# Where a graph layer's logarithms are taken: one activation over four tiles, or two inside an earlier stage

## The chip, the cores and the metric

The kernel runs on one core of a Trainium2 chip, in float32 for all large products. The metric is the device time of one execution in microseconds. A core has TensorE (PE, matmuls; its weight loads are listed apart as PEld), VectorE (DVE), ScalarE (ACT), GpSimd (POOL, which here mostly issues accumulating transfers), and SyncE (SP), which issues most of the transfers. Each engine works through its own instructions in the order in which they were written; engines wait for each other through semaphores.

## The reference

Two graph attention layers over 512 nodes, 768 features and 16,896 edges, the first with eight heads whose outputs are concatenated, then a residual sum and a layer norm. Cut to what matters:

```python
def gat_layer(x, W, a_s, a_d, b, edge_index, concat):
    h = (x @ W).reshape(n, H, C)
    src, dst = (edge_index[0], edge_index[1])
    alpha_s = jnp.einsum('nhc,hc->nh', h, a_s)
    alpha_d = jnp.einsum('nhc,hc->nh', h, a_d)
    e = jax.nn.leaky_relu(alpha_s[src] + alpha_d[dst], 0.2)
    m = jax.ops.segment_max(e, dst, num_segments=n)
    e = jnp.exp(e - m[dst])
    denom = jax.ops.segment_sum(e, dst, num_segments=n)
    alpha = e / (denom[dst] + 1e-16)
    out = jax.ops.segment_sum(h[src] * alpha[:, :, None], dst, num_segments=n)
    return out.reshape(n, H * C) + b
h = jax.nn.elu(gat_layer(x, W1, a_src1, a_dst1, b1, ...))   # 8 heads of 768
y = gat_layer(h, W2, a_src2, a_dst2, b2, ...)               # 1 head
return layernorm(x + y)
```

## The kernel before, in words

The graph becomes a dense 512 x 512 matrix of edge counts, built once with one-hot matmuls (L681) while head 0's projection runs. `cnt` holds it in four tiles of 128 destinations x 512 sources, `absent` a large number wherever a pair has no edge. Attention is then dense: for each tile, a row of logits (`lift`, L575, on ScalarE), the leaky ReLU (`leak`, L579, VectorE), the row minimum with the mask (`rank`, L584, VectorE) and the exponential (L588 or L590, ScalarE).

Head 0 multiplies the exponentials by the counts (`weigh`, L811). All later heads have the counts inside the exponent: `logarithms` (L596) replaces all of `cnt` by the logarithm of itself plus a tiny number, and `fold_count` (L601, VectorE) turns a tile into `absent` minus the logarithm. From then on `folded` is not empty, and `rank` adds `cnt` instead of `absent` and lets the exponential sum up the denominator as well.

The first layer runs head by head. Each head has three stages: `projection` (x times the head's W1; `by_thirds` in later heads), `mixed` (the aggregation, attention times projected features), and `second` (ELU of the aggregate times the head's rows of W2, summed up in `h2`). The products use Strassen-like schemes of seven parts, P1 to P7. In `second` each part has two halves of 128 rows, and each half takes six matmul records (L367), so a part takes twelve. P2 accumulates onto the PSUM banks of P1, P4 onto those of P7 and P3 onto those of P5, after `empty` has taken the first part out: for head 0 with copies on ScalarE (L458) for P1 and P2, on VectorE for P6 (L462), P7 and P4 (L460).

In the loop over `n` from 2 to 6 inside a head (P6, P7, P4, P5, P3), the matmuls m0 and m1 of part n are written first, then `leak` and `rank` of the next head's attention tile n - 2, the next tile's `lift`, then e0 and e1, which empty the banks, with `weigh` and `turn_out` of finished attention tiles between. `turn_out` (L831 and L834, ScalarE, and a transposing transfer at L836 on SP) and `turn_in` (L839, ScalarE) transpose the attention into `PT`.

Head 0's stages around the change: projection 1 ends (`beside`, n = 13) with `turn_in(3)` and the sums over `PT` that the aggregation needs (L883 to L886, VectorE). `mixed` then runs three rounds c = 0, 1, 2; each copies P1 out into u (L915, ScalarE), adds P6 and P7 (L919, L920), passes P2 to `elu` (two Relus, L848 and L849, and an Exp, L850, on ScalarE, then L851 on VectorE), subtracts w from P5 (L925), adds P4 (L928) and P3 (L930), with logits of the next head (L376) in between. P3's matmuls accumulate onto P5's bank and so wait for L925. L360 is the last of the sums that P4's weights need in `second`.

ScalarE evaluates functions from a table set. A load of another set (`ACT_TABLE_LOAD` in the profile) stands ahead of the first activation that needs it: ahead of L596 for the logarithm, ahead of the first L588 after it for the exponential, and ahead of L1279 for the square root.

Of the kernel before, what the change touches and what calls it, by code (L numbers as in the profile page):

```python
# [13 lines left out]
AF = mybir.ActivationFunctionType  # L14
# [23 lines left out]
def gat_pass(  # L38
# [16 lines left out]
    nc = tc.nc  # L55
# [4 lines left out]
    NT = N // P  # L60
# [192 lines left out]
    tiny = const.tile([P, 1], F32, name="tiny")  # L253
# [73 lines left out]
    cnt = keep.tile([P, NT, N], F32, name="cnt")  # L327
# [244 lines left out]
    def lift(h, t):  # L572

        q = BC[h] if 0 < h < H and t + 1 == NT else qpool.tile([P, N], F32, name="q")
        nc.scalar.activation(q, BC[h][:, :N], AF.Identity, bias=AL[h][1][:, t:t + 1], scale=-1.0)  # L575
        return q

    def leak(q):
        nc.vector.scalar_tensor_tensor(q, q, NEG_SLOPE, q, op0=ALU.mult, op1=ALU.min)  # L579

    def rank(q, t):

        nmax = small.tile([P, 1], F32, name="nmax")
        nc.vector.tensor_tensor_reduce(out=q, in0=q, in1=(cnt if folded else absent)[:, t, :], scale=1.0,  # L584
                                       scalar=-NO_EDGE / 2 if folded else -NO_EDGE, op0=ALU.add, op1=ALU.min, accum_out=nmax)
        if folded:
            dens[t] = small.tile([P, 1], F32, name="den")
            nc.scalar.activation(q, q, AF.Exp, bias=nmax, scale=-1.0, accum_out=dens[t])  # L588
        else:
            nc.scalar.activation(q, q, AF.Exp, bias=nmax, scale=-1.0)  # L590
        return q

    folded, dens = [], {}

    def logarithms():
        nc.scalar.activation(cnt, cnt, AF.Ln, bias=tiny)  # L596
        folded.append(True)

    def fold_count(t):

        nc.vector.tensor_tensor(cnt[:, t, :], absent[:, t, :], cnt[:, t, :], op=ALU.subtract)  # L601
# [15 lines left out]
    if not general:  # L617
# [12 lines left out]
        cps, done = {}, set()  # L630
# [207 lines left out]
    def turn_in(t):  # L838
        nc.scalar.copy(PT.rearrange("p s n -> p (s n)").bitcast(U16).rearrange("p (s n h) -> p s n h", s=NT, h=2)[  # L839
            :, :, t * P:(t + 1) * P, :], parted.pop(t).rearrange("p (h s d) -> p s d h", h=2, s=NT))  # L840

    def elu(h, c, z, cols, name, spare=None):

        j = h * DC + c
        n = z.shape[-1]
        neg = work.tile([P, n], F32, name=f"n{name}")
        pos = work.tile([P, n], F32, name=f"z{name}", bufs=3 if name == "r" else 2) if spare is None else spare
        nc.scalar.activation(neg, z, AF.Relu, bias=nb1T[:, j:j + 1], scale=-1.0)  # L848
        nc.scalar.activation(pos, z, AF.Relu, bias=b1T[:, j:j + 1])  # L849
        nc.scalar.activation(neg, neg, AF.Exp, scale=-1.0)  # L850
        return lambda: nc.vector.scalar_tensor_tensor(gT[:, c, cols], neg, -1.0, pos, op0=ALU.add, op1=ALU.add)  # L851
# [13 lines left out]
    def left_sums(h):  # L865
        hs = HS[h]
        a11, a12, a21, a22 = hs[:, :2, L], hs[:, 2:, L], hs[:, :2, R], hs[:, 2:, R]
        s1, s2, s4 = (gS.rearrange("p a k n -> p a (k n)")[:, j, :].rearrange("p (k n) -> p k n", k=2)
                      for j in range(3))
        tt = nc.vector.tensor_tensor  # L870
        return dict(P1=a11, P2=a12, P3=s4, P4=a22, P5=s1, P6=s2, P7=a21), [
            lambda: tt(s1, a21, a22, op=ALU.subtract),
            lambda: tt(s2, s1, a11, op=ALU.subtract),
            lambda: tt(a21, a11, a21, op=ALU.subtract),
            lambda: tt(s4, a12, s2, op=ALU.add),
        ]

    def right_sums():
        b11, b12, b21, b22 = PT[:, :2, near], PT[:, :2, far_], PT[:, 2:, near], PT[:, 2:, far_]
        t1, t2, t4 = pS[:, 0], pS[:, 1], pS[:, 2]  # L880
        tt = nc.vector.tensor_tensor
        return dict(P1=b11, P2=b21, P3=b22, P4=t4, P5=t1, P6=t2, P7=b12), [
            lambda: tt(t1, b11, b12, op=ALU.add),  # L883
            lambda: tt(t2, t1, b22, op=ALU.add),
            lambda: tt(b12, b12, b22, op=ALU.add),
            lambda: tt(t4, t2, b21, op=ALU.add),  # L886
        ]

    def mixed(h, A_, B_, fill):

        tt = nc.vector.tensor_tensor
        behind = []

        def some(n):
            for f in fill[:n]:
                f()
            del fill[:n]

        for c in range(HK):
            u = work.tile([P, HN], F32, name="u")  # L900
            w = work.tile([P, HN], F32, name="w")
            zr = work.tile([P, N], F32, name="zr", bufs=3)
            bank = {}

            def part(p, over=None):
                if over is None:
                    bank[p] = mm.tile([P, 512], F32, name="mm")
                else:
                    bank[p] = bank[over]
                for k in range(2):  # L910
                    nc.tensor.matmul(bank[p][:, :HN], A_[p][:, k, c * P:(c + 1) * P], B_[p][:, k, :],  # L911
                                     start=over is None and k == 0, stop=k == 1, skip_group_check=True)
                return bank[p][:, :HN]

            nc.scalar.copy(u, part("P1"))  # L915
            if behind:

                behind = behind[0]()
            tt(u, u, part("P6"), op=ALU.add)  # L919
            tt(w, u, part("P7"), op=ALU.add)  # L920
            for f in behind[:1]:
                f()
            near_l = elu(h, c, part("P2", over="P1"), near, "l")
            some(1)
            tt(zr[:, far_], part("P5"), w, op=ALU.subtract)  # L925
            for f in behind[1:]:
                f()
            tt(zr[:, near], u, part("P4", over="P7"), op=ALU.add)  # L928
            near_l()
            tt(u, part("P3", over="P5"), u, op=ALU.subtract)  # L930
            some(-(-len(fill) // (2 * (HK - c) - 1)))

            def others(c=c, u=u, zr=zr):
                return [elu(h, HK + c, zr, slice(0, N), "r", spare=zr), elu(h, c, u, far_, "l", spare=u)]
            behind = [others]
        return behind[0]()
# [30 lines left out]
    def reload_x():  # L967
        nc.sync.dma_start(gF[:, :RELOAD * 2 * TH], stored)

    AA, lsums = left_sums(0)  # L970
    BB, rsums = right_sums()
    some_logits = half_logits(1, 2)

    def give(t):
        weigh(q[t], t)
        turn_out(q[t], t)

    done = {n: (lambda n=n: pairs[n][1]()) for n in range(4, 13)}
    beside = {4: [lambda: give(0)], 5: [done[4]], 6: [done[5]], 7: [done[6], lambda: give(1)],
              8: [done[7], lambda: leak(q[3]), lambda: rank(q[3], 3), lambda: turn_in(0)], 9: [lambda: give(2), done[8]],  # L980
              10: [lambda: give(3), lambda: turn_in(1), done[9]], 11: [done[10], lsums[0]],
              12: [done[11], lambda: turn_in(2), *lsums[1:3]], 13: [done[12], lambda: turn_in(3), *rsums[:2]]}
    for n in range(4, 14):
        pairs[n][0]()
        for f in beside[n]:
# [25 lines left out]
    for h in range(H - 1):  # L1011
# [37 lines left out]
        pairs[3][1]()  # L1049
        last = h + 2 == H  # L1050
        if h == 0:
            logarithms()
            fold_count(0)
        q = [lift(h + 1, 0)]
        for n in range(2, 7):
            (m0, e0), (m1, e1) = pairs[2 * n:2 * n + 2]
            m0()
            if not last:
                m1()
            if n < 6:  # L1060
                leak(q[n - 2])
                rank(q[n - 2], n - 2)
            if n < 5:
                if h == 0:
                    fold_count(n - 1)
                q.append(lift(h + 1, n - 1))
            if last:

                if n > 4:
                    turn_in(n - 5)  # L1070
                if n == 6:
                    turn(q[2], 2)
                if n == 6:
                    weigh(q[3], 3)
                m1(lambda: turn(q[3], 3) if n == 6 else None)
            if not last and n == 6:
                turn_in(0)
                turn_out(q[2], 2, weigh(q[2], 2, scale=False))
            e0()
            if last and 2 < n < 6:  # L1080
                weigh(q[n - 3], n - 3)
                if n < 5:
                    turn_out(q[n - 3], n - 3)
            if not last and 3 < n < 6:
                turn_out(q[n - 4], n - 4, weigh(q[n - 4], n - 4, scale=False))
            if not last and n == 6:
                turn_out(q[3], 3, weigh(q[3], 3, scale=False))
                if 0 < h:
                    sums = rest_of_thirds()
                    reload_x()  # L1090
                load_w2(h + 1)()
            e1()
            for f in in_second[:1]:
                f()
            del in_second[:1]
            if 0 < h and not last and 2 < n < 6:
                attend[n - 3]()
# [223 lines left out]
```

## Time and profile before

| | us |
|---|---|
| median of 3 runs | 643.96 (642.9 to 644.09) |
| the profiled execution, its own time | 644.22 |
| its span | 642.4 |
| TensorE busy in the span | 629.8 |
| VectorE busy | 507.3 |
| ScalarE busy | 313.0 |
| L596, table load | 1.28 at 107.61 |
| L596, logarithm of 128 x 2048 | 2.00 at 108.90 |
| L601, four subtractions of 128 x 512 | 0.69 each, 110.93 to 119.4 |
| L588, table load | 1.28 at 111.53 |

Times inside the span count from its start. The profile's rows name the line, the engine, the operation, output <- input by the program's names, and sizes. In a timeline each row starts with its start and its duration; a bracket at the end holds the idle time of that engine just before and who ended it. "x12" merges twelve instructions. In a table of stretches, each row gives the stretch, its length, the busy time of PE, PEld, DVE, ACT and POOL with the number of instructions, the clock granted to TensorE as a share of full speed, the share of the DMA engines, and GB/s. In the list of waits a row gives the sum, the number and the longest.

Head 0's aggregation runs from 80.35 to 99, its second product from 99.17 to 130.6.

### The profile page before, as it was taken

Reading aid. Unit: us, or ns where it says so; the run is one execution under the profiler, and the core shown is the slowest. Engines: PE = TensorE matmul, PEld = TensorE weight load, DVE = VectorE, ACT = ScalarE, POOL = GpSimd, SP = SyncE. Lnnn points to the kernel's source line nnn. Section 1 sums busy time; section 2 is a strip of 40 time slices with the busy share of each in tenths; the row PEclk is TensorE's granted clock in tenths of the full one; section 3 lists DMA queues with packets and bytes.
Section 4 is the critical chain, followed back from the end, with each engine's and each line's share of the span. In section 5 each row is a group of like instructions: output and inputs, shape, how many; then the busy total and the mean of one; then the engine's idle time right before and its main releaser. Section 6 shows DMA issues by size and latency. Waiting matters only on the chain.

```text
span 642.4 us, 7641 instructions
## 1 busy us (share of the span) xinstructions
PE 629.8 (98%) x2509; PEld 436.9 (68%) x2509; DVE 507.3 (79%) x1079; ACT 313.0 (49%) x545; POOL 63.6 (10%) x105
## 2 busy tenths in 40 slices
PE   8999999899999999999999999999999999999995
PEld 5555586456856887588857886588857886645553
DVE  8989989688887878768787779668786878676675
ACT  5874657650637235560737245651728145543440
POOL 1300011010300202010300220010300110000000
PEclk9999999899999999999999999999999999999999
DMA  8993488586832978088924977088925990400122
GB/s 303 326 228 88 92 231 288 125 242 176 255 102 66 332 219 205 17 250 216 245 96 98 322 216 187 22 272 218 221 90 131 318 293 23 129 27 2 33 58 77
DMA packets 86844, 109.87 MB, mean 171 GB/s; under 512 B 40150, under 2 KB 67982, under 8 KB 86030
## 3 DMA queue, kind: packets, MB, share of 16 engines
q1 hardware_dynamic: 70590, 87.42, 40.8%
q0 software_dynamic: 15776, 21.30, 19.9%
q10 hardware_dynamic: 432, 0.59, 0.3%
q8 instruction: 22, 0.36, 0.2%
q14 instruction: 24, 0.20, 0.1%
HBM read 95.12 MB, written 2.90 MB: 153 GB/s over the span
## 4 chain that ended last, share of the span: by engine, by line
PE 94%; DVE 2%; ACT 1%; DMA 1%; issue 0%; SPq 0%; DVEq 0%; ACTq 0%
PE mm L367 43%; PE mm L426 20%; PE mm L911 18%; PE mm L857 3%; PE mm L1267 3%; PE held L367 2%; PE tr L681 1%; DMA q<-drow 1%; PE bc L234 1%; PE held L547 1%; PE bc L681 0%; ACT os L653 0%; PE mm L265 0%; ACT cnt L596 0%; PE tr L1191 0%
## 5 line engine op out<-in xcount | busy, mean ns | idle before, releaser
L367 PE MATMUL mm<-w,gT 128*128 128x384 f32 x252 | 83.6, 486 | 0.0
L367 PEld LDWEIGHTS mm<-w,gT 128*128 128x128 f32 x252 | 47.9, 190 | 31.9
L588 ACT ACTIVATE q<-q,nmax 128x512 f32<-128x512 f32 x32 | 23.1, 722 | 88.5 <-DVE nmax L584 88.5
L462 DVE TENSOR_TENSOR h<-h,mm 128x384 f32<-128x384 f32 x72 | 39.2, 551 | 31.1 <-PE mm L367 30.6
L432 ACT ACTIVATE hs<-mm 128x512 f32<-128x512 f32 x30 | 17.9, 597 | 91.2 <-PE mm L426 72.9
L911 PE MATMUL mm<-PT,hs 128*128 128x256 f32 x252 | 61.3, 379 | 0.0
L367 PE MATMUL mm<-w1t,gS 128*128 128x384 f32 x180 | 60.6, 487 | 0.0
L911 PEld LDWEIGHTS mm<-PT,hs 128*128 128x128 f32 x252 | 47.8, 190 | 7.2 <-ACT u L915 0.3
L367 PEld LDWEIGHTS mm<-w1t,gS 128*128 128x128 f32 x180 | 34.1, 190 | 24.0 <-DVE w1t L359 0.5
L434 DVE TENSOR_TENSOR hs<-hs,mm 128x512 f32<-128x512 f32 x45 | 30.8, 684 | 23.0 <-PE mm L426 23.0
L911 PE MATMUL mm<-pS,gS 128*128 128x256 f32 x168 | 43.1, 379 | 0.0
L839 ACT COPY PT<-zr 128x1024 uint16<-128x1024 uint16 x34 | 39.1, 1155 | 1.4 <-DMA zr<-pS 0.8
L426 PE MATMUL mm<-w2r,xT 128*128 128x256 f32 x160 | 37.8, 379 | 0.0
L426 PE MATMUL mm<-w2r,gT 128*128 128x256 f32 x160 | 37.5, 382 | 0.0
L367 PE MATMUL mm<-w1t,gT 128*128 128x384 f32 x96 | 34.2, 508 | 2.1 <-DVE h L460 2.1
L911 PEld LDWEIGHTS mm<-pS,gS 128*128 128x128 f32 x168 | 31.9, 190 | 4.3
L426 PEld LDWEIGHTS mm<-w2r,xT 128*128 128x128 f32 x160 | 30.4, 190 | 5.2
L426 PEld LDWEIGHTS mm<-w2r,gT 128*128 128x128 f32 x160 | 30.0, 190 | 5.8 <-DVE hs L434 1.9
L915 ACT COPY u<-mm 128x256 f32<-128x256 f32 x21 | 7.8, 373 | 49.0 <-PE mm L911 49.0
L655 DVE TENSOR_SCALAR os<-nodes,idx 128x512 bf16<-128x512 f16 x104 | 29.1, 351 | 1.4 <-PE tr L681 1.4
L367 PEld LDWEIGHTS mm<-w1t,gT 128*128 128x128 f32 x96 | 18.8, 198 | 16.3 <-DVE h L460 2.7
L367 PE MATMUL mm<-w,gS 128*128 128x384 f32 x84 | 28.6, 486 | 0.0
(241 smaller groups left out, 1265.7 us busy)
## 6 DMA issues: line engine op xcount, KB each, us to landing
w2r<-in_L_gnn_W_dram SPq DMA_DIRECT2D x48, 384.0 KB, 9.9
w<-in_L_gnn_W_dram SPq DMA_DIRECT2D x43, 384.0 KB, 11.0
gT<-xd SPq DMA_DIRECT2D x5, 1280.0 KB
w1t<-in_L_gnn_W_dram SPq DMA_DIRECT2D x9, 576.0 KB
w<-in_L_gnn_W_dram POOLq DMA_DIRECT2D x8, 576.0 KB, 8.7
w1t<-in_L_gnn_W_dram POOLq DMA_DIRECT2D x7, 576.0 KB, 9.7
w2t<-in_L_gnn_W_dram SPq DMA_DIRECT2D x15, 256.0 KB, 7.2
w2t<-in_L_gnn_W_dram POOLq DMA_DIRECT2D x15, 256.0 KB, 9.1
```

The source lines that it names most:

```text
L367: nc.tensor.matmul(ps[:, :HALF], A_[p][:, k, i * P:(i + 1) * P], B_[p][:, k, :], start=start and k == 0, stop=k == HK - 1, skip_group_chec ...
L426: nc.tensor.matmul(bank[chain][:, i * TH:(i + 1) * TH], A_[p][:, k, i * P:(i + 1) * P], B_[p][:, k, :], start=first and i == k == 0, stop= ...
L432: nc.scalar.activation(out(o), ps, AF.Copy, scale=how)
L434: nc.vector.tensor_tensor(out(o), out(o), ps, op=how)
L462: nc.vector.tensor_tensor(a, a, ps, op=ALU.subtract if p == "P7" else ALU.add)
L588: nc.scalar.activation(q, q, AF.Exp, bias=nmax, scale=-1.0, accum_out=dens[t])
L655: nc.vector.tensor_scalar(o, nodes, idx[:, c:c + 1], None, op0=ALU.is_equal)
L839: nc.scalar.copy(PT.rearrange("p s n -> p (s n)").bitcast(U16).rearrange("p (s n h) -> p s n h", s=NT, h=2)[:, :, t * P:(t + 1) * P, :], p ...
L857: nc.tensor.matmul(ps[:, :N], HS[h][:, s, c * P:(c + 1) * P], PT[:, s, :], start=(s == 0), stop=(s == NT - 1))
L911: nc.tensor.matmul(bank[p][:, :HN], A_[p][:, k, c * P:(c + 1) * P], B_[p][:, k, :], start=over is None and k == 0, stop=k == 1, skip_group ...
L915: nc.scalar.copy(u, part("P1"))
L1267: nc.tensor.matmul(ps[:, :cols.stop - cols.start], PT[:, s, t * P:(t + 1) * P], h2[:, s, cols], start=(s == 2), stop=(s == 1))
```

## The change

`logarithms()`, one activation over all four tiles, becomes `logarithm(tiles)`. It is called twice: for tile 0 at the end of projection 1, after `turn_in(3)`, and for tiles 1 to 3 in round 0 of head 0's aggregation, after u has been copied. The call in the second product goes. The subtractions of tiles 1 to 3 (`fold_count(n - 1)`) move in the loop from ahead of `lift` to behind e1.

```diff
-    def logarithms():
-        nc.scalar.activation(cnt, cnt, AF.Ln, bias=tiny)
+    def logarithm(tiles):
+        nc.scalar.activation(cnt[:, tiles, :], cnt[:, tiles, :], AF.Ln, bias=tiny)
         folded.append(True)
...
             nc.scalar.copy(u, part("P1"))
+            if h == c == 0:
+                logarithm(slice(1, NT))
             if behind:
...
-              12: [...], 13: [done[12], lambda: turn_in(3), *rsums[:2]]}
+              12: [...], 13: [done[12], lambda: turn_in(3), lambda: logarithm(slice(0, 1)), *rsums[:2]]}
...
         if h == 0:
-            logarithms()
             fold_count(0)
         q = [lift(h + 1, 0)]
         for n in range(2, 7):
...
             if n < 5:
-                if h == 0:
-                    fold_count(n - 1)
                 q.append(lift(h + 1, n - 1))
...
             e1()
+            if h == 0 and n < 5:
+                fold_count(n - 1)
             for f in in_second[:1]:
```

As built, ScalarE's order in the changed kernel is: `turn_in(3)`, a table load, the logarithm of 128 x 512, u's copy, the logarithm of 128 x 1536, the two Relus of L848 and L849, a table load, the Exp of L850, and on as before; in the second product the table load, the logarithm and the table load ahead of L588 are gone. TensorE's, SyncE's and GpSimd's instructions stand in the order they had.

## The prediction

> **What bounds the kernel now.** I read the shares of the page first, then the chain of waits, then the timeline around the logarithm.
>
> ```profile
> PE 629.8 (98%) x2509; PEld 436.9 (68%) x2509; DVE 507.3 (79%) x1079; ACT 313.0 (49%) x545; POOL 63.6 (10%) x105
> ...
> PE 94%; DVE 2%; ACT 1%; DMA 1%; issue 0%; SPq 0%; DVEq 0%; ACTq 0%
> ...
> PE mm L367 43%; PE mm L426 20%; PE mm L911 18%; PE mm L857 3%; PE mm L1267 3%; PE held L367 2%; PE tr L681 1%; DMA q<-drow 1%; PE bc L234 1%; PE held L547 1%; PE bc L681 0%; ACT os L653 0%; PE mm L265 0%; ACT cnt L596 0%; PE tr L1191 0%
> ```
>
> TensorE ends the chain for 94% of it, so time is won only where it stands or runs slowly. Its list of waits is short and holds one large place:
>
> ```profile
> PE mm L367 <- DVE h L460: 2.1, 1, 2.1
> ```
>
> One wait, in head 0's second product: P4 accumulates onto the banks of P7 and so waits until VectorE has copied P7 out (L460). The chain through that place, in order of time (start, us, what):
>
> ```profile
> 107.61 1.28 ACT L596
> ...
> 108.90 2.01 ACT cnt L596
> ...
> 110.93 0.69 DVE cnt L601
> ...
> 115.89 0.60 DVE cnt L601
> 116.50 0.48 DVE h L460
> ```
>
> The logarithm's table load, the logarithm and three subtractions (L601) stand ahead of the copy. What TensorE does then, and the granted clock there (column after POOL) in stretches of time:
>
> ```profile
> 117.02 5.83 PE L367 MATMUL mm<-w1t,gT 128*128 128x384 f32 x12 [2.09 <-DVE h L460]
> 122.69 4.03 PE L367 MATMUL mm<-w1t,gS 128*128 128x384 f32 x12
> ...
> 115.00:117.00 2.00, 0.00 (x0) 0.00 (x0) 1.97 (x6) 1.07 (x3) 0.00 (x0) 1.00 1.13 262
> 117.00:118.40 1.40, 1.38 (x4) 0.87 (x5) 1.37 (x3) 0.35 (x1) 0.00 (x0) 0.94 1.13 244
> 118.40:121.80 3.40, 3.40 (x7) 1.76 (x6) 1.80 (x6) 2.25 (x5) 0.00 (x0) 0.52 0.18 40
> ```
>
> So the place costs twice: 2.1 us of standing, and then twelve matmuls at 5.83 us where their neighbours take 4.03, since the clock is halved for 3.4 us. In stretches of 2 us over the whole span, the clock is below 1.00 nowhere else but after the last matmul.
>
> **The second product, term by term.** Groups of twelve matmuls start 3.87 us apart undisturbed (122.69 to 126.56). P7's started at 110.89, so P4's could at 114.76; it started at 117.02: 2.26 lost.
>
> (a) The wait for the logarithm. VectorE is free of L360 at 108.52 + 1.35 = 109.87 and idles 1.07 until 110.93 for the logarithm. With the logarithms long done, the first subtraction starts at 109.86: -1.07. The q tile it meets next (lift, L575) no longer stands behind load and logarithm either: it can start at 107.6 instead of 110.81.
>
> (b) Subtractions behind the evacuations. VectorE's order up to L460 was subtract, leak, rank, subtract, two L462, leak, rank, subtract, L460. By the diff the second subtraction goes behind the two L462, still ahead of the next leak, which gains nothing here; the third goes behind L460: -0.61 (start to start, 115.81 to 116.42). The moved ones fall into later idle time of VectorE: 0.67 ahead of the L460 at 120.09 and 1.97 ahead of that at 122.89, against 0.61 each. ScalarE's lifts must keep up: rank ends at 111.90, the exponential starts at 111.94, lift q1 runs 112.66 to 113.37 and leak wants it at 113.41; equal, so counted at nothing.
>
> So L460 starts at 116.42 - 1.68 = 114.74, P4's matmul 0.60 later (116.42 to 117.02) at 115.34, with 0.58 still lost. Head 1 has the same order without subtractions, starts P4 3.88 us after P7 (188.15 to 192.03) and loses nothing, which bounds this term at -2.26.
>
> (c) The clock. 5.83 - 4.03 = -1.80, if 0.58 us of idling does not halve it. A gap of 0.94 us before 14.24 has the clock at 1.00 on both sides; the gap that halved it is 2.09. 0.58 is below the smaller. The other end is 0. The Trainium skill, "TensorE: Matmul & The Clock Gate", section "What's actually happening", lets the clock fall only after an idle window of about 3.4 us; here 2.09 us of standing came before it, so the trace differs; if the fall had another cause than the standing, the 1.80 would stay, which is rival A.
>
> **Head 0's aggregation: what is added.** No DMA is issued or moved past on any queue; SP and POOL keep their order. ScalarE gets, after the last turn_in (L839, 78.36 to 79.52): a table load, 1.28 (L596's row), and Ln of tile 0. A 128x512 activation with a bias column takes 0.72 (L588, L848); 2048 columns of Ln took 2.00. End: 79.52 + 1.28 + 0.72 = 81.5, less the 0.09 by which successive activations overlap, 81.4. The next instruction, the copy of u (L915), started at 81.41 because it waited for P1: cost 0 to 0.1. Its cover is the 1.88 us of idle before it; without it the load and Ln would hold u, then L919 (slack 0.7, VectorE is at L886 until 82.64) and P2's matmuls. Ln of tiles 1 to 3, 1536 columns, between the two rows: 0.72 + 1.28 x 2/3 = 1.57, from 81.8 to 83.4, inside the 2.41 idle until L848 at 84.19: nothing.
>
> The table load back stands ahead of the first Exp (L850), since the Relus of L848 and L849 run before it. They end at 85.02; load to 86.32, Exp to 86.74 instead of 85.33. Behind it on VectorE, in order, stands L851 for gT, at 86.25 without idle: it goes to 86.78, +0.53. Behind that: L930 (0.1 of waiting swallowed), two L376, L919 at 89.00 becomes 89.34, L920 at 89.51 (waits for P7 0.17 of it) 89.68, L851 at 89.95, which waits for ScalarE's Exp until then, 90.03. L925 and with it the matmul of the second round's P3 (91.90), which writes onto the bank that L925 reads, are late by 0.1. That is this term: +0.1, with bounds 0 and +0.5.
>
> The load and the return load of the second product go: they were 107.61 to 108.89 and 111.53 to 112.81; the first is within (a), the second was hidden up to 0.15 behind rank.
>
> At this place a rule speaks against the change. The Trainium skill, "ScalarE: Activation LUTs", section "What ACT_TABLE_LOAD costs", states 1283 ns for the load and some 1380 ns of draining, 2.66 us in all for every switch. The trace agrees on the load (1283) and shows no draining: the copy ended at 107.59, the load began at 107.61, Ln at 108.90. By the page, both cushions above would be overrun; rival C works out a like case from rows.
>
> **Sum.** -1.07 - 0.61 - 1.80 + 0.1 = -3.4. The profiled execution took 644.22 us, span 642.4 and 1.8 around it, so 640.8; it stood 0.26 above the median of the runs shown (643.96), so 640.6. After 117 us TensorE waits for nothing over 0.4 us, so the gain should reach the end: loads are started by TensorE's releases and move along. Projection 2's weights, needed 3.4 us earlier (127.0), were asked for by 106.06, and the DMA engines stand at share 0.00 from 120 to 122.4, so they have landed.
>
> **The rivals.**
>
> A. The stall shrinks, but the half clock stays, because 0.58 us or something else suffices. For it: the point between 0.58 and 2.09 is not known at this place, and the fall came 1.4 us after the standing ended. Against: 0.94 us at 14.24 left no mark. Then 643.96 - 1.58 = 642.4.
>
> B. Another releaser takes over: VectorE or the lift reaches L460 later than the sum of starts says (the tie in b). For it: lift, leak and exponential of each tile follow one another with 0.04 between. Against: head 1 holds P4 with this chain. One exposed activation, 0.7, gives 641.3; it is inside my range.
>
> C. The slower side: a switch of tables costs the path twice its row, 2.57. Then u's copy goes to 82.7 and ends at 83.1, Ln runs to 84.6, the Relus to 85.3, the load back to 87.9, Exp to 88.3; L851 is 2.1 late, L925 1.66 late, and TensorE stands 1.66 at 91.9. That is nearer to 2.09 than to 0.94, so the clock halves there instead: +1.66 + 1.80 + 0.1 for P2 = 3.56 against the 3.48 gained: 644.1, slower. It decides from about 2.5 us per switch, and each further 0.1 adds 0.2 (both switches lie in the one line), so it passes 0.2% from 3.2 us. Against it: no gap around L596's load. The page's 2.66 would make it 644.2.
>
> D. It does not do what it says: the copy L460 is late for some reason other than the logarithm and P4 starts as before, 644.0. Against: the chain has nothing else in these 9 us.
>
> **How the numbers follow.** Forecast with B, 0.77; A, 0.10; C, 0.09; D, 0.04. This kernel's measurement can tell about 0.2%, 1.3 us, from no change. The predicted time is the likeliest's, 640.6. Low end: the second product loses nothing (-0.58) and another 0.4 us between measurements, 639.6. High end: A with 0.2 on top, 642.6; what is left above is C, D and a little of A. Faster by over 0.2% (below 642.67): 0.77 and half of A, 0.82. Within: the other half of A (0.05), D (0.04) and the part of C up to 3.2 us per switch (0.04), 0.13. Slower: the part of C beyond, which no row here caps, 0.05.
>
> **What would show it.** The load and Ln of tile 0 end before 81.5 and u's copy stays near 81.4; Ln of three tiles takes some 1.57; L851 is late by half a microsecond and P3's matmul of round two by 0.1; no idle before the first L601; P4's group starts 4.4 to 4.5 us after P7's and takes 4.03 with the clock at 1.00 throughout. It would be wrong if the list of waits gains an entry of TensorE on L925 or L851 over 1 us, if the clock falls anywhere before the end, or if the twelve matmuls of P4 still take 5.8.

## The result, and the profile after

| | before | changed |
|---|---|---|
| median, us (6 runs each) | 643.89 (642.9 to 644.09) | 640.76 (640.5 to 641.21) |
| ratio, with its 95% interval | | 0.9954 (0.9941 to 0.9966) |
| span of the profiled execution, us | 642.4 | 639.0 |

Of the 54 runs of the kernel before that stand beside the experiments, 18 took 642.68 to 643.34 us at a granted clock of 0.997 or 0.998 in the mean of the span and 36 took 643.67 to 644.50 at 0.995 or 0.996, with none between; the profile of before is of the second kind, and what the clock did at this place in the first kind was not profiled.

From TensorE's list of waits in the changed kernel (engine, line, tile, who it waited for, sum, times, longest; the changed file's lines are one or two further down):

```profile
PE mm L911 <- DVE zr L927: 0.6, 2, 0.4
...
PE mm L367 <- DVE h L460: 0.3, 1, 0.3
```

The wait on L460 has gone from 2.1 us to 0.3, and one on L927 (L925 before) in head 0's aggregation is new, 0.23 us; the other of the two is the one of 0.4 in a later head that was there before. The timeline of the changed kernel in the second product:

```profile
109.72 0.68 DVE L601 TENSOR_TENSOR cnt<-absent,cnt 128x512 f32<-128x512 bf16 x1
...
110.82 4.03 PE L367 MATMUL mm<-w,gT 128*128 128x384 f32 x12
...
114.57 1.01 DVE L460 TENSOR_SCALAR h<-mm 128x384 f32<-128x384 f32 x2
...
115.18 4.14 PE L367 MATMUL mm<-w1t,gT 128*128 128x384 f32 x12 [0.33 <-DVE h L460]
...
119.15 4.03 PE L367 MATMUL mm<-w1t,gS 128*128 128x384 f32 x12
```

The first subtraction waits for nobody. P4 starts 4.36 us after P7 (6.13 before), and the next group 3.97 after P4 (5.67 before). The stretches of time that held the half clock (the column after POOL is the granted clock):

```profile
117.00:118.40 1.40, 1.40 (x6) 0.85 (x5) 1.27 (x5) 0.79 (x3) 0.00 (x0) 1.00 1.12 243
118.40:121.80 3.40, 3.40 (x12) 1.96 (x11) 2.41 (x6) 2.29 (x4) 0.00 (x0) 1.00 0.15 38
```

And ScalarE at the seam of projection and aggregation, where the logarithms now stand:

```profile
79.23 1.28 ACT L596 ACT_TABLE_LOAD   x1
80.53 0.72 ACT L596 ACTIVATE cnt<-cnt,tiny 128x512 f32<-128x512 f32 x1
81.16 0.35 ACT L915 COPY u<-mm 128x256 f32<-128x256 f32 x1
81.41 1.58 ACT L596 ACTIVATE cnt<-cnt,tiny 128x1536 f32<-128x1536 f32 x1
83.88 0.47 ACT L848 ACTIVATE nl<-mm,nb1T 128x256 f32<-128x256 f32 x1 [0.90 <-PE mm L911]
...
84.74 1.28 ACT L850 ACT_TABLE_LOAD   x1
86.03 0.42 ACT L850 ACTIVATE nl<-nl 128x256 f32<-128x256 f32 x1
```

The rows give an account of the whole difference, in starts of TensorE's groups. The aggregation's first group started at 80.35 before and 80.04 now: 0.31 came earlier, from the first 6 us, where nothing was changed. From there to P3 of round 1: 11.55 before (80.35 to 91.90), 11.80 now (80.04 to 91.84), +0.25. P7 to P4: -1.77. P4 to the next: -1.70. Projection 2's first group: 130.43 before, 126.89 now, -3.54, and -0.31 + 0.25 - 1.77 - 1.70 = -3.53. The last product's first group starts at 614.80 and 611.27, again -3.53: nothing was given back on the way. The spans differ by 3.4, so about 0.1 went behind the last product.

### The profile page after: what moved, and what is told of

The parts are those of the page before. It is cut to its first block, busy times and chain, and to the rows that moved or that the text cites. A ratio compares the mean times of both kernels' runs of the same rounds, so it can differ in the third digit from the quotient of the medians.

```text
span 639.0 us, 7642 instructions
## 1 busy us (share of the span) xinstructions
PE 628.0 (98%) x2509; PEld 435.7 (68%) x2509; DVE 506.7 (79%) x1079; ACT 312.9 (49%) x546; POOL 63.6 (10%) x105
## 4 chain that ended last, share of the span: by engine, by line
PE 93%; DVE 4%; DMA 1%; ACT 1%; issue 0%; SPq 0%; DVEq 0%; ACTq 0%
PE mm L367 42%; PE mm L426 20%; PE mm L911 18%; PE mm L857 3%; PE mm L1268 3%; PE held L367 2%; PE tr L681 1%; DMA q<-drow 1%; DVE scr L376 1%; PE bc L234 1%; PE held L547 1%; PE bc L681 1%; DVE w1t L359 0%; ACT os L653 0%; DMA drow<-turned 0%
## 5 line engine op out<-in xcount | busy, mean ns | idle before, releaser
L588 ACT ACTIVATE q<-q,nmax 128x512 f32<-128x512 f32 x32 | 23.1, 722 | 91.0 <-DVE nmax L584 91.0
L367 PE MATMUL mm<-w1t,gT 128*128 128x384 f32 x96 | 32.5, 488 | 0.3 <-DVE h L460 0.3
L915 ACT COPY u<-mm 128x256 f32<-128x256 f32 x21 | 7.8, 371 | 46.0 <-PE mm L911 46.0
L834 ACT COPY pS<-q 128x1024 uint16<-128x1024 uint16 x26 | 27.1, 1044 | 2.6 <-DVE q L817 2.1
```

The source lines that it names most:

```text
L367: nc.tensor.matmul(ps[:, :HALF], A_[p][:, k, i * P:(i + 1) * P], B_[p][:, k, :], start=start and k == 0, stop=k == HK - 1, skip_group_chec ...
L834: nc.scalar.copy(apart.rearrange("p (h n) -> p h n", h=2), q.bitcast(U16).rearrange("p (n h) -> p h n", h=2))
```

## The experiments

Each kernel ran beside the kernel before; times are medians. The start of the aggregation lies between 80.0 and 81.1 us from one profile to the next, because the first 9 us of matmuls and transposes vary; so stages are compared by their own starts, and differences of a few tenths between medians are not read.

**The logarithms alone.** The changed kernel with `fold_count(n - 1)` back in its old place:

```diff
             if n < 5:
+                if h == 0:
+                    fold_count(n - 1)
                 q.append(lift(h + 1, n - 1))
...
-            if h == 0 and n < 5:
-                fold_count(n - 1)
```

> The logarithms moved as in the change, the subtractions left ahead of the lifts as before. My account: the subtraction of tile 2 stands ahead of L460 again, so L460 starts 0.61 us later than in the changed kernel, P4's first matmul 4.97 us after P7's (4.36 in the changed kernel, 6.13 before), 1.1 us lost against the 3.87 of an unhindered group. 1.1 is nearer to the 0.94 us gap that left the clock alone than to the 2.09 that halved it, so the clock stays at 1.00: ratio to before 0.9962, about 641.4. Rival A (less standing suffices to halve it): P4's twelve matmuls take 5.7 again and the ratio is 0.9988, about 643.1.

Measured: 641.22, ratio 0.9967 (0.9955 to 0.998). Its timeline:

```profile
111.50 4.03 PE L367 MATMUL mm<-w,gT 128*128 128x384 f32 x12
116.47 4.14 PE L367 MATMUL mm<-w1t,gT 128*128 128x384 f32 x12 [0.93 <-DVE h L460]
120.44 4.03 PE L367 MATMUL mm<-w1t,gS 128*128 128x384 f32 x12
```

4.97 as expected, and 3.97 to the next group: standing 0.93 us left the clock alone here. The move of the third subtraction is worth the 0.61 between 4.97 and 4.36.

**The subtractions alone.** The kernel before with `fold_count(n - 1)` behind e1:

```diff
             if n < 5:
-                if h == 0:
-                    fold_count(n - 1)
                 q.append(lift(h + 1, n - 1))
...
             e1()
+            if h == 0 and n < 5:
+                fold_count(n - 1)
```

> The subtractions moved behind the evacuations, the one logarithm left in the second product. My account: the wait of 1.07 us for the logarithm stays, L460 starts 0.61 earlier than before, P4's first matmul 5.5 us after P7's, 1.65 lost. If the clock halves at that (1.65 is nearer to 2.09 than to 0.94): -0.6, ratio 0.9991, about 643.3. If it does not, -2.3, ratio 0.9964, about 641.6. In either case the aggregation keeps its times of before.

Measured: 641.78, ratio 0.9971 (0.996 to 0.9983). Its timeline:

```profile
110.57 4.03 PE L367 MATMUL mm<-w,gT 128*128 128x384 f32 x12
116.10 4.14 PE L367 MATMUL mm<-w1t,gT 128*128 128x384 f32 x12 [1.49 <-DVE h L460]
120.07 4.03 PE L367 MATMUL mm<-w1t,gS 128*128 128x384 f32 x12
```

The start came as expected (5.53), but the clock stayed whole: 1.49 us of standing was still too little here, and of the two outcomes that I had priced, the one that I had leaned away from came true. So moving 0.61 us of work saved 2.3 us in the rows and 2.0 between the medians. It also means that the two parts do not add up: 0.33% and 0.29% alone, 0.40 to 0.46% together, since either one removes the 1.70 of half clock.

**The wait kept, the engine kept busy.** The kernel before, with two matmuls whose result nobody reads:

```diff
             (m0, e0), (m1, e1) = pairs[2 * n:2 * n + 2]
+            if h == 0 and n == 4:
+                spare = bc.tile([P, 512], F32, name="bc")
+                for _ in range(2):
+                    nc.tensor.matmul(spare, ident, xT[:, 0, :], start=True, stop=True)
             m0()
```

> The kernel before with nothing moved; two matmuls of 128x512 whose result nobody reads are written ahead of P4 in head 0, so that TensorE works while it waits. By the rows (384 columns every 0.3225 us, two records to a matmul) they take 1.72 us, inside the 2.09 of waiting. My account (the half clock comes from standing): P4 starts 6.13 us after P7 as before, and its twelve matmuls take 4.03 instead of 5.83 with the clock at 1.00: -1.7, ratio 0.9974, about 642.2. Rival (the half clock at 118.4 has another cause than the standing): P4 takes 5.8 and the ratio is 1.000.

Measured: 642.18, ratio 0.9977 (0.9968 to 0.9986). Its timeline (L1060 are the added matmuls):

```profile
110.58 4.03 PE L367 MATMUL mm<-w,gT 128*128 128x384 f32 x12
114.45 1.88 PE L1060 MATMUL bc<-xT,ident 128*128 128x512 f32 x4
116.72 4.14 PE L367 MATMUL mm<-w1t,gT 128*128 128x384 f32 x12 [0.38 <-DVE h L460]
120.69 4.03 PE L367 MATMUL mm<-w1t,gS 128*128 128x384 f32 x12
```

P4 starts 6.14 us after P7, as late as ever, and yet the next group follows after 3.97. The half clock was an effect of the standing, worth 1.70, and it can be had back without touching the wait.

**The wait put back into the changed kernel.** Three subtractions on VectorE that nobody reads:

```diff
+            if h == 0 and n == 3:
+                for cols in (slice(0, N), slice(0, N), slice(0, HN)):
+                    nc.vector.tensor_tensor(scr[:, cols], absent[:, 0, cols], cnt[:, 0, cols], op=ALU.subtract)
             e0()
```

> The changed kernel with three subtractions on VectorE whose results nobody reads (two of 128x512, one of 128x256) ahead of L460, so that P4 waits again though the logarithms are where the change put them. By the rows they take 0.61 + 0.61 + 0.35: P4 starts 5.9 us after P7, 2.05 lost, TensorE stands some 1.9 us, between the 1.49 that left the clock at 1.00 and the 2.09 that halved it. My account (standing alone halves it, from somewhere between): if it halves, 1.57 + 1.7 above the changed kernel, 644.2; if not, 1.57 above, 642.5; both in turn from run to run would say that the point lies here. Rival (the logarithm in the second product had part in the half clock): never halved.

Measured: 644.57, ratio 1.0008 (0.9999 to 1.0017). Its timeline:

```profile
114.91 1.87 DVE L1080 TENSOR_TENSOR scr<-absent,cnt 128x512 bf16<-128x512 bf16 x3
...
117.31 5.83 PE L367 MATMUL mm<-w1t,gT 128*128 128x384 f32 x12 [2.12 <-DVE h L460]
122.98 4.03 PE L367 MATMUL mm<-w1t,gS 128*128 128x384 f32 x12
```

The three took 1.79 to the next start instead of 1.57, so the standing came out at 2.12 instead of 1.9, as long as in the kernel before, and everything of it is back: 5.67 us between the groups, clock 0.51 from 118.4 to 121.8. The placing of the logarithm has no part in that. It is therefore no finer bound on the length that suffices; that lies between 1.49 and 2.09 and was not narrowed further. Of its 11 runs seven took 644.29 to 645.05 at a mean granted clock of 0.995 or 0.996, three 643.59 to 643.69 at 0.997 and one 642.67 at 0.999, which would fit a clock that is not halved every time; only one of the seven was profiled, so this stays open.

**Two more switches of tables.** Behind the logarithm of tiles 1 to 3:

```diff
                 logarithm(slice(1, NT))
+                back = small.tile([P, 2], F32, name="back")
+                nc.scalar.activation(back[:, :1], ones, AF.Exp)
+                nc.scalar.activation(back[:, 1:], ones, AF.Ln)
```

> The changed kernel with two further switches of tables behind the logarithm of tiles 1 to 3: an Exp and a Ln of one column each, whose results nobody reads, each with its load ahead. It makes rival C by force. My account (a switch costs its load of 1.28 and nothing more, a tiny activation 0.29): the two Relus of round 0 start 2.2 us later, at 86.1, the Exp ends at 88.6, L851 is 2.2 late against the changed kernel, and TensorE waits about 2.1 us for L927 at round 1's P3 (91.8), which halves the clock there too: 2.1 + 1.7 on top of the changed kernel, 644.5, ratio 1.001. If a switch cost 2.6, as rival C had it, the Relus would start 4.8 late and the ratio would be 1.005 or more. If the slack of the aggregation took it up, the ratio would be 0.996 as in the changed kernel.

Measured: 644.59, ratio 1.0013 (1.0003 to 1.0022). Its timeline from the first added load on:

```profile
84.36 1.28 ACT L919 ACT_TABLE_LOAD   x1
...
85.66 0.20 ACT L919 ACTIVATE back<-ones 128x1 f32<-128x1 f32 x1
85.86 1.28 ACT L920 ACT_TABLE_LOAD   x1
...
89.85 0.43 DVE L851 SCALAR_TENSOR_TENSOR gT<-nl,zl 128x256 f32<-128x256 f32 x1 [2.45 <-ACT nl L850]
...
93.40 1.13 PE L911 MATMUL mm<-pS,hs 128*128 128x256 f32 x4 [1.27 <-DVE w L925]
...
95.21 1.13 PE L911 MATMUL mm<-PT,gS 128*128 128x256 f32 x4 [0.69 <-DVE zr L930]
```

A switch cost its load: from 84.36 to 85.66 is 1.30, and so is the next (85.86 to 87.16). L851 is 2.0 us later after L915 of its round than in the changed kernel, and TensorE stands for it, as expected, but in two pieces, 1.27 at P4 and 0.69 at P3 (L925 and L930 of this kernel are L920 and L925 of the one before; that P4 writes onto the bank that w is read from, and so waits as well, I had left out). From the aggregation's start to the second product's it took 21.40 us against 19.06 in the changed kernel: for these waits P4 and P3 of round 1 start 2.0 later than there, and the other 0.34 was lost at the first groups (see the next experiment). In this profile the clock stays at 1.00 and the run took 644.05, so the half clock that I had expected on top is not in it. Of the ten runs five took 644.84 to 645.43 at a mean granted clock of 0.995 or 0.996 (0.997 in the profiled one), which would fit a half clock there; but such a mean also came with a clock that was whole to the last matmul (0.996 in the kernel below that turns the sign on ScalarE and has a tiny Exp), and none of the five was profiled. So the waiting of rival C is real, 2.0 us for two switches; that its half clock follows is not shown, and a switch did not cost the 2.57 that it needs.

**The table brought back early.** The changed kernel with a tiny Exp ahead of the Relus:

```diff
                 logarithm(slice(1, NT))
+                nc.scalar.activation(small.tile([P, 1], F32, name="back"), ones, AF.Exp)
```

> The changed kernel with an Exp of one column behind the logarithm of tiles 1 to 3, so that the table comes back in ScalarE's 0.90 us of idle ahead of the Relus instead of ahead of the Exp that L851 waits for. My account: load from 82.9 to 84.2, tiny Exp to 84.5, the Relus start 0.6 later than in the changed kernel, the Exp of round 0 ends near 85.7 instead of 86.45, L851 follows L930 with no wait, and the 0.25 us that the change added to the aggregation goes: 0.1 to 0.3 us below the changed kernel, which the times can hardly tell and the rows can (round 1's P3 0.2 earlier). Rival: the later Relus hold P2's bank and cost as much again, no gain in the rows.

> The changed kernel beside the next three on one chip: ratio to before 0.995, P4 4.36 us after P7, its twelve matmuls 4.14, L851 of round 0 waiting 0.45 for the Exp.

Measured, beside each other: 641.16, ratio 0.9961 (0.9947 to 0.9974), and 641.20, ratio 0.996 (0.9946 to 0.9973). In the rows, L851's wait for the Exp and the new wait of TensorE on L927 are gone. But `turn_in(2)` waited 0.26 for its transfer, `turn_in(3)` came later against P1, and TensorE lost 0.34 at the aggregation's first groups instead (they start 1.02 and 1.16 apart, not 0.87 and 0.97), so that P3 of round 1 started 11.90 after the aggregation (11.80 in the changed kernel beside it). The same 0.34 stands in the profiles of all four kernels here that have an added activation of one column, and in none of the other ten profiles: it came with the edit, and why is not shown. In the rows the edit thus lost 0.1 on the whole, and the medians do not tell the two kernels apart.

**The subtractions on GpSimd.** In the changed kernel, all four `fold_count` behind the logarithm of tiles 1 to 3, as `nc.gpsimd.tensor_tensor`:

```diff
-        nc.vector.tensor_tensor(cnt[:, t, :], absent[:, t, :], cnt[:, t, :], op=ALU.subtract)
+        nc.gpsimd.tensor_tensor(cnt[:, t, :], absent[:, t, :], cnt[:, t, :], op=ALU.subtract)
...
                 logarithm(slice(1, NT))
+                for t in range(NT):
+                    fold_count(t)
```

> The changed kernel with all four subtractions given to GpSimd, right behind the logarithm of tiles 1 to 3. No row here has such an operation on GpSimd; tile 0 is wanted at 110 and the work can start at 83, so up to 6 us each would do. My account: VectorE reaches L460 1.22 us earlier, P4 starts 3.9 after P7 with nothing lost, 0.49 us below the changed kernel: ratio 0.9943. Rival: GpSimd and VectorE hinder each other in the aggregation, where VectorE is busy for 16.4 of 19 us; VectorE's rows there grow and TensorE waits for L927: same or slower than the changed kernel.

> Both of the above: 0.7 us below the changed kernel if both accounts hold, ratio 0.9940, about 640.0.

Measured: 645.76, ratio 1.0036 (1.0024 to 1.0047); with the tiny Exp as well, 645.5, ratio 1.0034 (1.0024 to 1.0044). The first one's timeline:

```profile
85.42 5.00 POOL L601 TENSOR_TENSOR cnt<-absent,cnt 128x512 f32<-128x512 bf16 x4
85.88 0.42 DVE L932 TENSOR_TENSOR zr<-u,mm 128x256 f32<-128x256 f32 x1 [0.44 <-PE mm L911]
86.75 3.96 DVE L851 SCALAR_TENSOR_TENSOR gT<-nl,zl 128x256 f32<-128x256 f32 x1 [0.45 <-ACT nl L850]
...
93.83 1.71 PE L911 MATMUL mm<-pS,hs 128*128 128x256 f32 x4 [2.81 <-DVE w L924]
```

L851, 0.42 us in the changed kernel, lasts until all four operations of GpSimd are through. TensorE stands 2.81 us, and its clock is 0.53 from 94.0 to 97.6. Farther on it did what it was for, P4 started 3.98 after P7 and waited for nobody. The rival that I had named for it won, though TensorE waited for w (L924) at P4 and not for the subtraction at P3 that it named.

**The subtractions on ScalarE.** The changed kernel without them; the sign is turned in ScalarE's idle time:

```diff
-        if h == 0:
-            fold_count(0)
         q = [lift(h + 1, 0)]
+        if h == 0:
+            for t in (0, 2):
+                nc.scalar.activation(cnt[:, t:t + 2, :], cnt[:, t:t + 2, :], AF.Copy, scale=-1.0)
...
-            if h == 0 and n < 5:
-                fold_count(n - 1)
```

> The changed kernel without subtractions: ScalarE turns the sign of the logarithms in place, two copies of 128x1024 with scale -1 behind lift 0 in the second product, where it has 3.6 us of idle. Pairs without an edge then get 41 added (the logarithm of 1e-18) instead of 1e30. My account: VectorE's first leak starts at L360's end, L460 is held by the lift of q1 and starts about 0.6 earlier than in the changed kernel, P4 starts 3.87 after P7 with nothing lost: 0.49 us below the changed kernel, 640.6 if that takes 641.1. Rival (the tie with the lifts, B of the prediction): P4 still loses 0.2 or more.

> The same with the tiny Exp behind the logarithm of tiles 1 to 3, which gave round 1's P3 back its start: 0.7 us below the changed kernel in the rows, ratio to before 0.9945 if the changed kernel has 0.9955.

> The changed kernel beside the next three on one chip: ratio to before 0.995 to 0.996.

Measured, beside each other: 640.38, ratio 0.9950 (0.9936 to 0.9963); with the tiny Exp 640.61, ratio 0.995 (0.9937 to 0.9964); the changed kernel 641.05, ratio 0.9957 (0.9943 to 0.997). The first one's timeline:

```profile
111.82 4.03 PE L367 MATMUL mm<-w,gT 128*128 128x384 f32 x12
...
113.73 0.69 DVE L579 SCALAR_TENSOR_TENSOR q<-q 128x512 f32<-128x512 f32 x1 [0.56 <-ACT q L575]
...
115.69 4.14 PE L367 MATMUL mm<-w1t,gT 128*128 128x384 f32 x12
```

P4 follows P7 after 3.87 and waits for nobody; VectorE now waits 0.56 for the lift of q1, which is the tie of rival B, with nothing behind it that TensorE needs sooner. In the rows it is 0.49 better than the changed kernel; the medians differ by 0.67, and the intervals overlap, so that it beats the changed kernel is shown for this stage and not by the times. The premise of the kernel with the tiny Exp, that it had given round 1's P3 back its start, was wrong (11.90 above); P3 started 11.91 after the aggregation here too.

## Why the prediction was right, point by point

- **What bounds.** Right: one wait of TensorE carried the whole change, and what was won there arrived at the last product untouched.
- **Terms (a) and (b), L460 earlier by 1.07 and 0.61.** Right: P4 was to lose 0.58 and lost 0.49. The 0.61 is confirmed by the logarithms alone (4.97 against 4.36), the 1.07 by the subtractions alone (5.53 against 4.36). That is 1.17, since VectorE starts an instruction some 0.08 before the listed end of the one ahead when nothing holds it, as at 109.72 in the changed kernel, where L360 is listed from 108.45 for 1.35; I had counted from the listed end, and this is most of the 0.09.
- **Term (c), the clock, -1.80.** The cause is shown by the kernel that kept TensorE busy through the wait and by the one that put the wait back. The size was 0.1 too large: I had taken busy times (5.83 and 4.03), where starts of groups give 5.67 and 3.97, 1.70 in the profiled executions. Rival A, that 0.58 or less would halve it too, fell: 1.49 does not.
- **The aggregation, +0.1.** Mis-sized: +0.25, within its bounds. L851 was late by 0.54 (0.53 forecast) and L930 by 0.36 (0.34), both against the aggregation's start. The step that failed is the next one, "L920 at 89.51 (waits for P7 0.17 of it) 89.68": that pause was not slack. L920 reads the u that L919 writes, and the two start 0.51 to 0.52 apart in both kernels (the first two rows are of before, the others of the changed kernel, where the lines are two further down), so it came 0.35 late; only the 0.1 ahead of L851 was there to take up any of it.

```profile
89.00 0.41 DVE L919 TENSOR_TENSOR u<-u,mm 128x256 f32<-128x256 f32 x1
89.51 0.42 DVE L920 TENSOR_TENSOR w<-u,mm 128x256 f32<-128x256 f32 x1
...
89.03 0.41 DVE L921 TENSOR_TENSOR u<-u,mm 128x256 f32<-128x256 f32 x1
89.55 0.42 DVE L922 TENSOR_TENSOR w<-u,mm 128x256 f32<-128x256 f32 x1
```

- **The table loads.** Right: u's copy started 1.12 us after P1 (1.06 before), the logarithm of three tiles took 1.58 (1.57 forecast). The load ended at 80.51 and the logarithm began at 80.53; the other ended at 86.02 and the Exp began at 86.03. The Trainium skill, "ScalarE: Activation LUTs", section "What ACT_TABLE_LOAD costs", adds some 1380 ns of draining to each switch; neither these two nor the two added ones show it.
- **The sum.** -3.4 was forecast and -3.2 is what the terms measured; 640.6 against 640.76. The 0.1 of the clock and the 0.15 of the aggregation were too hopeful, and the 0.09 of the wait was too careful, so a little of the closeness is luck. The 0.31 by which the aggregation started earlier in the profile belongs to no term.

## What to carry to other kernels

A short wait of TensorE can be worth more than its length: here about two microseconds of standing cost another 1.70 at half clock, and any one of three edits (0.6 us less waiting, 1.2 us less, or useless matmuls in the gap) took that back in its profile, so price the parts of such a change together and not one by one. A pause between two instructions of one engine where the second reads what the first wrote need not be slack: here it was none. Work that is moved to an idle engine has to be asked what it shares with the busy one: the subtractions' work cost nothing in its stage on ScalarE, and on GpSimd 4.6 us against the changed kernel beside it.

## What the runs showed of the hardware

GpSimd's subtraction, 128x512 with two inputs in SBUF, is listed with 1.65 us; four of them started some 1.1 us apart, their rows overlapping, and took 5.00 us together. Meanwhile a VectorE operation with two SBUF inputs stood from 86.75 to 90.71 (and for 4.20 us in the kernel with the tiny Exp), whereas L932, with one input in SBUF and one in PSUM, took its usual 0.42. The Trainium skill, "SBUF — State Buffer", section "SBUF: two separate sides", says that a VectorE instruction with two SBUF inputs and a GpSimd instruction that reads SBUF exclude each other for a whole instruction; the trace agrees, and adds that VectorE did not get in between GpSimd's successive instructions.

The clock's half stretches lasted 3.4 us each. They followed waits of 2.09, 2.12, 2.51 and 2.81 us, and none followed waits of 0.93 and 1.49, nor 1.27 and 0.69 within 3.4 us, in one profile each. They began 0.4 to 1.2 us after the wait had ended, not at its end; whether it matters where a wait lies in time was not varied, so 1.49 and 2.09 are bounds for these executions and no rule. The Trainium skill, "TensorE: Matmul & The Clock Gate", section "What's actually happening", has a window of that length but asks for a whole idle one; about 60% of one was enough here.
